# Graph attention over 16 batches: mask transfers issued from ScalarE's queue half a batch earlier, mask flags on GpSimd, one self-feature bank seeded with flags

## The chip, the cores and the metric

The kernel runs on one core of a Trainium2 chip. The metric is the device time of one execution in microseconds. Engines are named as in the profile: PE (TensorE's matmuls; PEld its weight loads), DVE (VectorE), ACT (ScalarE), POOL (GpSimd) and SP (SyncE, which here only issues transfers). A q behind an engine's name (SPq, ACTq) means its sequencer, which issues DMAs.

## The reference

Sixteen graphs of 512 nodes with 512 features. Each node attends to the first 20 nodes with 16 heads, in two directions of a labelled adjacency (11 labels):

```python
def _gat_attention(self_feat, cond_adj, label_bias, Wq, bq, Wk, bk, Wout, bout):
    kv = self_feat[:, :ng]                                  # ng = 20 of 512 nodes
    qh = (self_feat @ Wq.T + bq).reshape(B, N, H, dh)       # H = 16, dh = 32
    kh = (kv @ Wk.T + bk).reshape(B, ng, H, dh)
    aff = jnp.einsum('bnhd,bmhd->bnhm', qh, kh) * (1.0 / np.sqrt(dh))
    aff = jnp.where(cond_adj[:, :, None, :] > 0, aff, NEG) + label_bias[:, :, None, :]
    w = jax.nn.softmax(aff, axis=-1)
    out_t = jnp.einsum('bnhm,bmf->bnhf', w, kv)
    return (jnp.einsum('bnhf,hgf->bnhg', out_t, Wout) + bout.reshape(H, F // H)).reshape(B, N, F)

row_zero = v.sum(-1) == 0                                   # v: 16 x 512 x 512, q: 16 x 512
vcq = jnp.concatenate([v, jnp.where(row_zero[..., None], 0.0, q[:, None, :])], axis=-1)
self_feat = vcq @ W_self.T + b_self
output = self_feat
for d in range(2):
    A = (adj_f if d == 0 else jnp.swapaxes(adj_f, 1, 2))[:, :, :20, :]
    output = output + _gat_attention(self_feat, A.sum(-1), A @ w_bias + b_bias, ...)
return v + relu(output)
```

## The kernel before, in words

**Setup** (the first 105 us or so). The weights come in; the key rows of all batches are computed and multiplied with Wq in bursts numbered n = 0 to 21 (function `keys`), whose results (`st`, copied from PSUM by ACT and DVE) go to `g_d` in DRAM, from where each batch loads its key tensor `g`. Between the bursts stand the other setup jobs, by a table `plan` of letters, one word for a burst, and by a few lines `if n == ...`: the biases, the row sums of Wq times the bias (`bias_terms`, L671, on DVE, of the first four bursts), the value rows, self_feat of batch 0 (letter s), and the masks of batch 0 (first multiplies, count, flags, sum, spread).

**The loop.** One table `ORDER` lists the steps of a turn, each with a batch offset: `S7+0` is step S7 of this turn's batch, `F1+1` step F1 of the next one, `O-1` the last step of the batch before. The loop over turns issues the steps in that order; each engine executes its own instructions in the order in which they were issued, and semaphores are set where data passes between engines. So a step that waits holds back all that stands behind it on its engine. DMAs are issued by an engine's instruction stream too, before the change nearly all by SP; the transfers share eight completion counters in turn, and one whose counter is still in use waits for the earlier one.

**What a turn does.**
- Scores: seven half-size products S1 to S7 (`scores`, L412, 64 matmuls each) of the node features (blocks `sf`, sums `z` made by POOL in steps Z) with the keys (blocks of `g`, differences `y` made by POOL in steps Y). They are accumulated in two PSUM pairs, `pair_a` (S1, S4, S6, S7) and `pair_d` (S2, S3, S5). Before a use, a pair is seeded by ACT: `sa` (L432) and `sc` (L438) copy the bias scores `cq`, **`sd` (L436) copies the mask `both` into `pair_d`**.
- Taking the results: `t11`, `t22` (L443, ACT copies out of `pair_a`), `m22` (L452, POOL adds the mask `both`), `f11`, `f22` (L456, DVE adds `pair_d`), `t12`, `f21` (L448).
- Softmax of the four tiles 11, 12, 21, 22: maximum `mx` (L463, DVE), subtraction `sub` (L467, POOL), `exp` (L471, ACT), `sum` (L475, DVE), `rec` (L478, DVE), `nor` (L482, POOL), `turn` (L489, DVE).
- Attention: `O` (L507, PE) on banks into which ACT has copied self_feat (`so`, L493); `oe` (L518, DVE, then a DMA) adds the input and stores.
- The next batch's self_feat: seven products F1 to F7 (`product`, L279; sums `t` of the input by POOL, steps X) into PSUM `banks`: F1, F4, F6 and F7 accumulate in bank 0, F2 in bank 1, F3 and F5 in bank 2. The partial sums `p1` to `p4` (`partial`, L311, DVE) read bank 0 after F1, F6, F7 and F4, and add `nq`, which is the flag of non-zero rows times the q part (steps `nq`, L301, four ACT operations of 128x512); `j1` to `j3` (`joined`, L317, DVE) add the other banks. As bank 0 goes on being accumulated, **F6 waits for `p1`**.
- The next batch's mask: `mul0` to `mul10` (L339, ACT) multiply the eleven labels with their biases into `prod`, `cnt` (L344, DVE) counts the labels, `flg` (L347, DVE) turns the count into 0 or -9e15 in a twelfth column of `prod`, `msum` (L351, DVE) sums over the twelve, and `spr` (`mask_spread`, L362) has eight DMAs on SP that spread the sum `add` over the partitions of `both`, as the PSUM layout needs it:

```python
for pg in range(2):
    for hp in range(2):
        for t in range(2):
            nc.sync.dma_start(adds[b][bass.ts(2 * pg + hp, R), :, 2 * t : 2 * t + 2], add[bass.ts(2 * pg + t, R)])
```

In the order of the turn, S7, F1, S4, F6, F5, F7, S3, F2, F3, F4, S1, S2, S6, S5, O is PE's work from S7 on.

Of the kernel before, what the change touches and what calls it, by code (L numbers as in the profile page):

```python
# [31 lines left out]
def gat_kernel(  # L32
# [223 lines left out]
    def product(b, n):  # L256
# [12 lines left out]
        for i in range(2):  # L269
            for k in range(2):  # L270
                wide = k == 0 and n in (1, 2, 3)
                mov = x_half(b, {1: 0, 2: 1, 3: 1}[n], int(n == 3))[:, 0] if wide else x[:, k]
                for a in range(HL):
                    at = i * P + a * R
                    if isinstance(w, tuple):
                        lhs = ws_v[:, 2 * w[1] + k, bass.ds(w[0] * F // 2 + at, R)]
                    else:
                        lhs = ws_s[:, w, k, bass.ds(at, R)]
                    nc.tensor.matmul(  # L279
                        to[bass.ts(a, R), i] if wide else to[bass.ts(a, R), i, :, HK:], lhs, mov,  # L280
                        start=n in (1, 2, 5) and (i, k) == (0, 0), stop=k == 1, skip_group_check=True,
                    )
# [17 lines left out]
    def flag_row(to, b, c):  # L300
        ran(nc.scalar.activation(to, nzs[b], AF.Identity, bias=bo[:, c : c + 1], scale=qw[:, c, b : b + 1]))  # L301
# [5 lines left out]
    def partial(b, n):  # L307

        new_self(b)
        f, l = {1: (0, 0), 2: (0, 1), 3: (1, 1), 4: (1, 0)}[n]  # L310
        ran(nc.vector.tensor_add(block(b, f, l), of_bank(0), by_half(nqs[b, f])[:, :, :, l, HK:]))  # L311
# [14 lines left out]
    def first_masks():  # L326
        a = adjs[0].rearrange("p t (m l) -> p (t m) l", l=L)
        p = new_prod(0)
        nc.scalar.copy(p[:, :, :L], a)
        nc.gpsimd.tensor_mul(p[:, :, :L], p[:, :, :L], wb_sb.unsqueeze(1).to_broadcast([P, 4 * S, L]))  # L330
# [15 lines left out]
    def mask_flag(b):  # L346
        ran(nc.vector.tensor_scalar(new_prod(b)[:, :, L], conds.pop(b), 0.0, NEG, ALU.is_le, ALU.mult))  # L347
# [7 lines left out]
    def mask_spread(b):  # L355
# [3 lines left out]
        for pg in range(2):  # L359
            for hp in range(2):  # L360
                for t in range(2):
                    nc.sync.dma_start(  # L362
# [159 lines left out]
    with tc.tile_pool(name="setup", bufs=1) as sp, tc.tile_pool(name="ps_acc", bufs=4, space=PSUM) as acc["pool"]:  # L522
# [19 lines left out]
        with tc.tile_pool(name="setup_k", bufs=1) as sk:  # L542
# [132 lines left out]
            def biases():  # L675

                nc.vector.tensor_add(bqw, bqw, bq_sb)
                for hl in range(HL):
                    nc.vector.tensor_copy(bqbd[bass.ts(hl, DH), :, :, hl], bqw[bass.ts(hl, DH)])
                nc.vector.tensor_add(bo, bo_sb[:, 0], bo_sb[:, 1])  # L680
                nc.vector.tensor_add(bo, bo, bs_sb)
                nc.vector.tensor_scalar(bqn, bqbd[:, :, :2], -1.0, None, ALU.mult)
# [3 lines left out]
        with tc.tile_pool(name="setup_g", bufs=4) as sg:  # L686
# [96 lines left out]
            def self_step(b, f, h, i, k):  # L783
# [9 lines left out]
                "b": [(biases, ())],  # L793
# [9 lines left out]
            plan = "bvv vv vv ccw vv ns ssss sssw vv vv ssss ssss vv vv nww ssss ssss".split()  # L803
# [13 lines left out]
            for n, runs in enumerate(bursts):  # L817
# [12 lines left out]
                if n == 7:  # L830
                    first_masks()
                if n == 9:
                    mask_count(0)
                if n == 10:
                    load_cq(0)
                    mask_flag(0)
                if n == 11:
                    row_sums(1)
                if n == 13:
# [16 lines left out]
    with tc.manual_schedule():  # L856
# [3 lines left out]
        for t in (pair_a[:, 0], pair_a[:, 1], pair_d[:, 0], pair_d[:, 1], banks[3]):  # L860
# [4 lines left out]
            "kv": kv_copy, "cnt": mask_count, "flg": mask_flag, "msum": mask_sum, "spr": mask_spread,  # L865
            "rm": row_mask, "O": attend,
        }
        for c in range(C):
# [4 lines left out]
            steps[f"nq{c}"] = lambda b, c=c: flag_rows(b, c)  # L873
            steps[f"rs{c}"] = lambda b, c=c: row_sum(b, c)
# [19 lines left out]
        for ij in (11, 12, 21, 22):  # L894
            lower_on = nc.vector if ij in LOWER_V else nc.gpsimd
            steps[f"t{ij}"] = lambda b, ij=ij: (take_masked if ij == 12 else take)(b, ij)
# [10 lines left out]
        def first(name):  # L907
# [5 lines left out]
            if name[0] in "FXpj" or name[:2] in ("nq", "La", "LG", "Lc", "mu") or name in (  # L913
                "cnt", "flg", "msum", "spr", "kv"
# [63 lines left out]
```

## Time and profile before

| what | value |
|---|---|
| time, median of 2 runs | 643.05 us (641.56 to 644.55) |
| the profiled execution | 644.64 us, span 642.9 us |
| granted TensorE clock, mean | 0.962 |
| busy: PE, PEld, DVE, ACT, POOL | 571.8, 437.1, 453.3, 323.4, 446.6 us |
| instructions: PE, DVE, ACT, POOL | 13784, 660, 618, 380 |
| mean DMA rate | 203 GB/s |

The span is the time between the first and the last instruction that the profiler shows. Busy times of different engines overlap. In a row of the profile, "L311 DVE TENSOR_TENSOR sf<-ps_o,nq 128x492" is line, engine, operation, what is written and read, and the shape; "[1.48 <-PE ps_o L279]" is how long the engine stood idle before the instruction and what ended that; "x8" counts instructions. Batch 0 is computed in the setup, turn 0 begins at about 105 us, and the stretches of the prediction run from the end of one `O` to the end of the next, the first at 168.3 us.

### The profile page before, as it was taken

The numbers are of one execution on the slowest core, as the hardware profiler recorded it, in microseconds if no ns is written. First come the engines' busy times: TensorE is split into PE (matmuls) and PEld (weight loads), VectorE is DVE, ScalarE is ACT, GpSimd is POOL, SyncE is SP. The second block draws the span as 40 slices with busy tenths as digits, with TensorE's granted clock in tenths as the row PEclk, the third lists the DMA queues.
The fourth block names the chain that finished last, engine by engine and source line by source line (L and its number), as shares of the span: only waits on it lengthen the run. The fifth ranks groups of instructions, "written<-read, shape, count | busy, mean of one in ns | idle before, by whom it ended". The sixth has DMA issues, their size and how long they took to land.

```text
span 642.9 us, 30976 instructions
## 1 busy us (share of the span) xinstructions
PE 571.8 (89%) x13784; PEld 437.1 (68%) x13785; DVE 453.3 (71%) x660; ACT 323.4 (50%) x618; POOL 446.6 (69%) x380
## 2 busy tenths in 40 slices
PE   9979997739999899999898899999999898999952
PEld 5434444626887688777676677679877876898941
DVE  1385762417878678878785888777888787788763
ACT  1414332805656465656473756464756565664321
POOL 2304645527979687878796889787888786889841
PEclk9989999778999989999999999999999999999995
DMA  8978779975757585757575767576868575745022
GB/s 300 390 281 303 268 285 358 276 172 165 211 169 218 164 221 171 221 178 215 161 214 175 196 196 206 181 205 185 225 180 232 155 218 167 215 124 157 9 84 67
DMA packets 121031, 130.49 MB, mean 203 GB/s; under 512 B 31585, under 2 KB 93057, under 8 KB 118849
## 3 DMA queue, kind: packets, MB, share of 16 engines
q1 hardware_dynamic: 119648, 126.62, 64.5%
q8 instruction: 108, 1.77, 1.2%
q0 software_dynamic: 672, 1.36, 1.0%
q10 hardware_dynamic: 576, 0.53, 0.2%
q14 instruction: 27, 0.21, 0.1%
HBM read 85.97 MB, written 40.24 MB: 196 GB/s over the span
## 4 chain that ended last, share of the span: by engine, by line
PE 42%; DMA 16%; ACT 14%; SPq 11%; DVE 8%; issue 3%; POOL 3%; POOLq 0%; DVEq 0%; ACTq 0%
PE ps_o L279 11%; PE ps_a L412 11%; PE ps_d L412 8%; PE ps_o L507 6%; DMA xn<-in_xn 5%; SPq L362 5%; ACT prod L339 5%; DMA both<-add 3%; ACT ps_o L493 3%; DMA x<-in_xT 2%; PE ps_v L725 2%; SPq L174 2%; DMA adj<-in_adj 1%; PE ps_sf L217 1%; ACT s L471 1%
## 5 line engine op out<-in xcount | busy, mean ns | idle before, releaser
L482 POOL TENSOR_TENSOR s<-s,sum 128x640 f32<-128x640 f32 x64 | 80.9, 1274 | 55.9 <-DVE sum L478 55.8
L412 PE MATMUL ps_a<-y,z 128*32 128x152 f32 x2048 | 77.6, 302 | 19.7 <-ACT s L443 18.1
L339 ACT ACTIVATE prod<-adj,wb_sb 128x160 f32<-128x160 int32 x165 | 90.7, 589 | 7.6 <-DMA adj<-in_adj 7.6
L467 POOL TENSOR_TENSOR s<-s,top 128x640 f32<-128x640 f32 x64 | 81.5, 1275 | 16.1 <-DVE top L463 14.7
L279 PE MATMUL ps_o<-t,ws_s 128*32 128x246 f32 x1440 | 80.7, 376 | 11.7 <-DVE sf L311 11.7
L412 PEld LDWEIGHTS ps_a<-y,z 128*32 128x32 f32 x2048 | 66.9, 113 | 30.7 <-issue 28.7
L471 ACT ACTIVATE s<-s 128x640 f32<-128x640 f32 x64 | 47.0, 734 | 66.1 <-POOL s L467 66.0
L412 PE MATMUL ps_d<-g,z 128*32 128x152 f32 x2048 | 73.8, 295 | 5.0 <-ACT ps_d L438 3.3
L475 DVE TENSOR_REDUCE sum<-s 128x32 f32<-128x640 f32 x64 | 51.9, 812 | 36.1 <-ACT s L471 36.1
L279 PEld LDWEIGHTS ps_o<-t,ws_s 128*32 128x32 f32 x1440 | 54.6, 111 | 32.3 <-DVE sf L311 14.7
L412 PEld LDWEIGHTS ps_d<-g,z 128*32 128x32 f32 x2048 | 66.3, 111 | 10.9 <-ACT ps_d L438 6.3
L311 DVE TENSOR_TENSOR sf<-ps_o,nq 128x492 f32<-128x492 f32 x60 | 40.1, 668 | 36.7 <-PE ps_o L279 36.7
L507 PE MATMUL ps_o<-wt,vd 32*32 32x256 f32 x2048 | 48.0, 400 | 11.6 <-ACT ps_o L493 6.8
L279 PE MATMUL ps_o<-x,ws_v 128*32 128x256 f32 (+1 forms) x960 | 58.3, 375 | 0.0
L301 ACT ACTIVATE nq<-nz,bo,qw 128x512 f32<-128x512 f32 x64 | 51.8, 812 | 6.0 <-DVE nz L207 6.0
L489 DVE STREAM_TRANSPOSE wt<-s 128x640 f32<-128x640 f32 x64 | 53.4, 834 | 1.7 <-POOL s L482 1.6
L456 DVE TENSOR_TENSOR s<-ps_d,s 128x640 f32<-128x640 f32 x48 | 39.2, 817 | 20.3 <-POOL s L452 11.9
L436 ACT COPY ps_d<-both 128x640 f32<-128x640 f32 x16 | 11.1, 697 | 80.1 <-DMA both<-add 40.3
L463 DVE TENSOR_REDUCE top<-s 128x32 f32<-128x640 f32 x64 | 50.4, 790 | 0.0
L518 DVE SCALAR_TENSOR_TENSOR o<-ps_o,x 128x512 f32<-128x512 f32 x64 | 40.1, 670 | 11.5 <-PE ps_o L507 11.4
L493 ACT COPY ps_o<-sf 128x512 f32<-128x512 f32 x64 | 36.4, 583 | 21.7 <-DVE o L518 20.2
L507 PEld LDWEIGHTS ps_o<-wt,vd 32*32 32x32 f32 x2048 | 29.5, 105 | 25.9 <-issue 7.7
(246 smaller groups left out, 1156.6 us busy)
## 6 DMA issues: line engine op xcount, KB each, us to landing
g<-g_d SPq DMA_DIRECT2D x60, 304.0 KB, 3.3
g_d<-st SPq DMA_DIRECT2D x16, 1064.0 KB, 5.8
out_T<-o SPq DMA_DIRECT2D x64, 256.0 KB, 4.6
xn<-in_xn SPq DMA_DIRECT2D x56, 256.0 KB, 5.3
x<-in_xT SPq DMA_DIRECT2D x56, 256.0 KB, 4.2
adj<-in_adj SPq DMA_DIRECT2D x32, 440.0 KB, 4.5
vd<-bd_d SPq DMA_DIRECT2D x64, 64.0 KB, 3.3
nz<-nz_d SPq DMA_DIRECT2D x14, 256.0 KB, 4.1
```

The source lines that it names most:

```text
L279: nc.tensor.matmul(to[bass.ts(a, R), i] if wide else to[bass.ts(a, R), i, :, HK:], lhs, mov, start=n in (1, 2, 5) and (i, k) == (0, 0), st ...
L301: ran(nc.scalar.activation(to, nzs[b], AF.Identity, bias=bo[:, c : c + 1], scale=qw[:, c, b : b + 1]))
L339: ran(nc.scalar.activation(new_prod(b)[:, :, l], a[:, :, l], AF.Identity, scale=wb_sb[:, l : l + 1]))
L412: nc.tensor.matmul(to[bass.ts(q, R)], rows[:, k, q // 2, bass.ds((2 * t + u) * R, R)], keys[:, k, q % 2], start=False, stop=k == 1, skip_g ...
L463: ran(nc.vector.tensor_reduce(tops[b, ij], flat(soft_tile(b, ij)), AX.X, ALU.max))
L467: ran(engine.tensor_sub(s, s, tops.pop((b, ij)).unsqueeze(2).to_broadcast([P, 4 * 2 * HL, NG])))
L471: ran(nc.scalar.activation(s, s, AF.Exp))
L475: ran(nc.vector.tensor_reduce(tops[b, ij], flat(soft_tile(b, ij)), AX.X, ALU.add))
L482: ran(engine.tensor_mul(s, s, tops.pop((b, ij)).unsqueeze(2).to_broadcast([P, 4 * 2 * HL, NG])))
L489: ran(nc.vector.transpose(wts[b][:, j, i], soft_t.pop((b, ij)).rearrange("p v h m -> p (v h m)")))
L493: ran(nc.scalar.copy(banks[q].rearrange("p (j n) -> p j n", j=2), of_out(sfs[b], hp, pg)))
L507: nc.tensor.matmul(banks[q][bass.ts(e, DH), bass.ts(j, NH)].rearrange("p (v r) -> p v r", r=R), vds[b][r, j, e, i], w[:, :, bass.ts(block, ...
```

## The change: what moves where

1. The eight DMAs of `mask_spread` are issued by ACT instead of SP, and the step `spr` stands right behind `t22` and `Lxn0`, before `sum11`, where it stood before between `sa` and `mx21`, after F6.
2. `prod` has eleven columns instead of twelve. The flags are made in place on the count by POOL (`flg`), and a new step `madd` on POOL adds them to the sum of `msum`.
3. With `P1_A`, bank 1 is treated like the pairs (one more marking matmul ahead of the loop): ACT writes flags times q for half of the nodes into it (`nd0`, `nd1`, 128x256 each), F2 accumulates onto that, and `nq0`, `nq1` write the other half only (128x2x128). `p1` is two ACT copies (128x2x123 each) of bank 0, in place of the DVE addition.
4. In the setup `bias_terms` leaves the first four bursts for later ones (letter t), the output bias is a job of its own (letter o), biases, bias scores, masks, `row_sums(1)` and `weight_sums` move to later bursts, and the spread of batch 0 is issued by ACT at n = 18 instead of by SP at n = 15.
5. `ORDER` is written anew in many places: in turn 0 and all others `m22` stands ahead of `Y2` on POOL, and `sd` ahead of `mul0` of the next batch on ACT.

ACT around the place where the eight DMAs go, an ordinary turn, first before, then after. `s_22` is tile 22 (L443 and L460 are `t22`), `xn` the row sums, `nz` the flags, `qw` the q part, L493 and L510 are `so`, L432 and L449 `sa`.

```order
L185 ACTIVATE xn_0_2025,rs_2554<-xn_0_2025 128x512
L443 COPY s_22_2587<-ps_a 128x640 [waits DVE_49,PE_49]
L185 ACTIVATE xn_2_2069,rs_2554<-xn_2_2069 128x512 x2
L493 COPY ps_o_1174<-sf_1946 128x512 [waits DVE_49]
L432 COPY ps_a<-cq_2392 128x4x160 [waits DMAHW6_49,DMAHW5_49,DMAHW7_49,DMAHW0_49,DVE_49]
L471 ACTIVATE s_21_2639<-s_21_2639 128x640 [waits Pool_49]
L471 ACTIVATE s_22_2587<-s_22_2587 128x640 [waits Pool_49]
L339 ACTIVATE prod_2782<-adj_2517,wb_sb 128x160 [waits DMAHW6_49,DMAHW2_49]
L436 COPY ps_d<-both_2667 128x4x160 [waits DMAHW4_49,DMAHW3_49,DMAHW5_49,DMAHW2_49,DMAHW6_49,DMAHW1_49,DMAHW7_49,DMAHW0_49,DVE_49]
```

```order
L460 COPY s_22_2030<-ps_a 128x640 [waits DVE_49,PE_49]
L379 DMA both_2034<-add_1954 32x2x80 [waits DMAHW3_49,Pool_49]
L379 DMA both_2034<-add_1954 32x2x80 [waits DMAHW4_49]
L379 DMA both_2034<-add_1954 32x2x80 [waits DMAHW6_49]
L379 DMA both_2034<-add_1954 32x2x80 [waits DMAHW0_49]
L379 DMA both_2034<-add_1954 32x2x80 [waits DMAHW1_49]
L379 DMA both_2034<-add_1954 32x2x80 [waits DMAHW3_49]
L379 DMA both_2034<-add_1954 32x2x80 [waits DMAHW5_49]
L379 DMA both_2034<-add_1954 32x2x80 [waits DMAHW6_49]
L310 ACTIVATE ps_o_1173<-nz_1638,bo,qw 128x256 [waits DVE_49]
L322 COPY sf_1990<-ps_o_1172 128x2x123 [waits PE_49]
L322 COPY sf_1990<-ps_o_1172 128x2x123
```

The eight DMAs, each with a wait for its completion counter (DMAHW), now stand between `t22` and the three instructions of `nd0` and `p1`; before, ACT went on to `so` and `sa` after `t22` and two row sums, and the seed waited for all eight counters.

PE behind S4 (L412 and L429, the rows with `y_4`), first before, then after; `ps_o_1171` and `ps_o_1172` are bank 0, `ps_o_1173` and `ps_o_1174` bank 2, `t_2` marks F6, `t_1` F5, `t_3` F7:

```order
L279 MATMUL ps_o_1171<-x_2663,ws_v 32x2x123 x4
L412 MATMUL ps_a<-y_4_2760,sf_2512 32x8x19 [waits Activation_49]
L412 MATMUL ps_a<-y_4_2760,sf_2512 32x8x19 x31
L279 MATMUL ps_o_1171<-t_2_3124,ws_s 32x2x123 [waits DVE_49,Pool_49]
L279 MATMUL ps_o_1171<-t_2_3124,ws_s 32x2x123 x15
L279 MATMUL ps_o_1173<-t_1_3075,ws_s 32x2x123 x16
L279 MATMUL ps_o_1171<-t_3_3004,ws_s 32x2x123 [waits DVE_49]
```

```order
L429 MATMUL ps_a<-y_4_3876,sf_3700 32x8x19 [waits Activation_49]
L429 MATMUL ps_a<-y_4_3876,sf_3700 32x8x19 x31
L281 MATMUL ps_o_1172<-t_2_4276,ws_s 32x2x123 [waits Activation_49,Pool_49]
L281 MATMUL ps_o_1172<-t_2_4276,ws_s 32x2x123 x15
L281 MATMUL ps_o_1174<-t_1_4228,ws_s 32x2x123 [waits DVE_49]
L281 MATMUL ps_o_1174<-t_1_4228,ws_s 32x2x123 x15
L281 MATMUL ps_o_1172<-t_3_4232,ws_s 32x2x123 [waits DVE_49]
```

PE's order is the same; F6's wait has gone from DVE to ACT.

POOL in turn 0, first before, then after: `y_2` is Y2, which needs the keys `g`, and `s_22<-s_22,both` is `m22`.

```order
L254 TENSOR_TENSOR t_2_1435<-x_174,t_1_1386 128x492
L254 TENSOR_TENSOR t_4_1441<-x_174,t_2_1435 128x492
L393 TENSOR_TENSOR y_2_1464<-g_1168 128x608
L452 TENSOR_TENSOR s_22_1459<-s_22_1459,both_941 128x640
L189 TENSOR_SCALAR nz_2_1527<-rs_1431 128x4
L482 TENSOR_TENSOR s_11_1279<-s_11_1279,sum_11_1466 128x640
```

```order
L370 TENSOR_TENSOR add_1393<-add_1393,cond_1243 128x160
L256 TENSOR_TENSOR t_4_1460<-x_174,t_2_1435 128x492
L469 TENSOR_TENSOR s_22_1462<-s_22_1462,both_1024 128x640
L410 TENSOR_TENSOR y_2_1516<-g_1169 128x608
L499 TENSOR_TENSOR s_11_1278<-s_11_1278,sum_11_1475 128x640
L484 TENSOR_TENSOR s_22_1462<-s_22_1462,top_22_1543 128x640
```

`m22` has passed Y2, and `madd` (L370) has come in three places ahead of Y2.

The diff, its core:

```diff
-                wide = k == 0 and n in (1, 2, 3)
+                wide = k == 0 and n in ((1, 3) if P1_A else (1, 2, 3))
...
-                        start=n in (1, 2, 5) and (i, k) == (0, 0), stop=k == 1, skip_group_check=True,
+                        start=n in ((1, 5) if P1_A else (1, 2, 5)) and (i, k) == (0, 0), stop=k == 1, skip_group_check=True,
...
-        flag_row(nqs[b, f][:, i], b, c)
+        if P1_A and f == 0:
+            flag_row(by_half(nqs[b, f])[:, i, :, 1], b, c, 1)
+        else:
+            flag_row(nqs[b, f][:, i], b, c)
+
+    def flag_bank(b, c):
+        flag_row(banks[1].rearrange("p (i g n) -> p i g n", i=2, g=2)[:, c], b, c, 0)
...
+        if P1_A and n == 1:
+            for i in range(2):
+                ran(nc.scalar.copy(block(b, f, l)[:, i], of_bank(0)[:, i]))
+            return
         ran(nc.vector.tensor_add(block(b, f, l), of_bank(0), by_half(nqs[b, f])[:, :, :, l, HK:]))
...
-            prods[b] = msk.tile([P, 4 * S, L + 1], F32, tag="prod", name=f"prod{b}", bufs=1)
+            prods[b] = msk.tile([P, 4 * S, L], F32, tag="prod", name=f"prod{b}", bufs=1)
...
-        ran(nc.vector.tensor_scalar(new_prod(b)[:, :, L], conds.pop(b), 0.0, NEG, ALU.is_le, ALU.mult))
+        ran(nc.gpsimd.tensor_scalar(conds[b], conds[b], 0.0, NEG, ALU.is_le, ALU.mult))
...
-    def mask_spread(b):
+    def mask_add(b):
+        t = conds[b, "sum"].rearrange("p t m -> p (t m)")
+        ran(nc.gpsimd.tensor_add(t, t, conds.pop(b)))
+
+    def mask_spread(b, queue=nc.scalar):
...
-                    nc.sync.dma_start(
+                    queue.dma_start(
...
-            plan = "bvv vv vv ccw vv ns ssss sssw vv vv ssss ssss vv vv nww ssss ssss".split()
+            plan = "ovvt vvt vvt wtt vvt nst ssst ssswb vvcc vv ssss ssss vv vv nww ssss ssss".split()
...
-                    for d in range(2):
-                        bias_terms(d, n)
...
-                if n == 15:
+                if n == 17:
                     mask_sum(0)
+                if n == 18:
+                    mask_add(0)
                     mask_spread(0)
```

More of the change, by code (lines that the diff above doesn't have):

```diff
@@ L864, in gat_kernel @@
             "clr": lambda b: clear_blocks(zero), "blk": lambda b: blocks(),
[L865 removed]
+            "kv": kv_copy, "cnt": mask_count, "flg": mask_flag, "msum": mask_sum, "madd": mask_add, "spr": mask_spread,
             "rm": row_mask, "O": attend,
@@ L895, in gat_kernel @@
             lower_on = nc.vector if ij in LOWER_V else nc.gpsimd
-            steps[f"t{ij}"] = lambda b, ij=ij: (take_masked if ij == 12 else take)(b, ij)
+            steps[f"t{ij}"] = lambda b, ij=ij: (take_masked if ij == 12 or ij == 22 and T22_V else take)(b, ij)
             steps[f"m{ij}"] = lambda b, ij=ij: mask_tile(b, ij)
@@ L912, in first @@
                 return range(2, B)
-            if name[0] in "FXpj" or name[:2] in ("nq", "La", "LG", "Lc", "mu") or name in (
-                "cnt", "flg", "msum", "spr", "kv"
+            if name[0] in "FXpj" or name[:2] in ("nq", "nd", "La", "LG", "Lc", "mu") or name in (
+                "cnt", "flg", "msum", "madd", "spr", "kv"
             ):
```

45 lines of the change are left out of this document (24 added, 21 removed).

## The prediction

> **What bounds the kernel now.** First the page's busy times and its chain of work that ended last.
>
> ```profile
> PE 571.8 (89%) x13784; PEld 437.1 (68%) x13785; DVE 453.3 (71%) x660; ACT 323.4 (50%) x618; POOL 446.6 (69%) x380
> PE 42%; DMA 16%; ACT 14%; SPq 11%; DVE 8%; issue 3%; POOL 3%; POOLq 0%; DVEq 0%; ACTq 0%
> L436 ACT COPY ps_d<-both 128x640 f32<-128x640 f32 x16 | 11.1, 697 | 80.1 <-DMA both<-add 40.3
> ```
>
> TensorE (PE) is busy 89% of the span, yet the chain stands on it for only 42%: it also passes through transfers (16%), ScalarE (ACT) and SyncE's issuing (SPq, 11%). The group says where: the seed copy L436 (step `sd`), which puts the mask `both` into PSUM, waits on the mask transfers. Next, the stretches from one end of `O` to the next, a turn each.
>
> ```profile
> 363.00:393.00 30.00, 29.32 (x799) 23.35 (x790) 25.38 (x36) 19.07 (x38) 25.45 (x22) 1.00 0.72 208
> 425.50:458.00 32.50, 30.87 (x848) 27.43 (x848) 25.48 (x36) 19.15 (x39) 26.14 (x22) 1.00 0.67 189
> 554.60:584.10 29.50, 29.50 (x804) 25.83 (x808) 25.29 (x35) 17.89 (x33) 24.44 (x21) 1.00 0.61 171
> 584.10:613.20 29.10, 29.10 (x804) 25.65 (x808) 20.86 (x34) 8.63 (x13) 22.48 (x18) 1.00 0.18 55
> sum 444.90, PE 418.59 PEld 349.44 DVE 349.73 ACT 254.67 POOL 359.11; mean PE 29.90 PEld 24.96 DVE 24.98 ACT 18.19 POOL 25.65
> ```
>
> Columns: length, then busy time of PE, its loads, DVE, ACT and POOL. The 14 turns sum to 444.90, 31.8 each. The last two have no PE idle: 29.50 with all engines loaded, 29.10 as the work runs out. So a turn without stalls costs 29.5, and 14 of them 12 x 29.5 + 2 x 29.1 = 412.2: **32.7 us of the loop are stalls**. No other engine has more than 26 us of work in a turn, so they come from order. One ordinary turn, from the timeline:
>
> ```profile
> 427.75 1.35 PE L412 MATMUL ps_a<-y,z 128*32 128x152 f32 x36
> 428.91 2.02 PE L279 MATMUL ps_o<-x,ws_v 128*32 128x256 f32 x32
> 429.16 0.69 ACT L443 COPY s<-ps_a 128x640 f32<-128x640 f32 x1 [2.83 <-PE ps_a L412]
> 429.95 1.50 SPq L521 DMA_DIRECT2D out_T<-o  x3
> 430.61 2.26 PE L412 MATMUL ps_a<-y,sf 128*32 128x152 f32 x62
> 430.98 0.67 DVE L311 TENSOR_TENSOR sf<-ps_o,nq 128x492 f32<-128x492 f32 x1 [1.48 <-PE ps_o L279]
> 431.54 2.53 SPq L128 DMA_DIRECT2D xn<-in_xn  x3
> 432.82 5.16 PE L279 MATMUL ps_o<-t,ws_s 128*32 128x246 f32 x94
> 436.50 6.91 SPq L362 DMA_DIRECT2D both<-add  x8
> 444.87 0.70 ACT L436 COPY ps_d<-both 128x640 f32<-128x640 f32 x1 [5.48 <-DMA both<-add]
> ```
>
> S7 ends at 429.1 (427.75 + 1.35), ACT takes its result (`t22`, 429.16); PE does F1 and S4; F6 follows at 432.8 at once, since DVE cleared bank 0 (`p1`, 430.98) meanwhile. SP issues the eight mask transfers at 436.5 to 443.4, the seed waits 5.48 us for them, and what stands behind the seed on ACT is late: the PE stalls of this turn come after it.
>
> **The change, step by step.** *The wait it removes.* With the transfers issued at 429.2 instead of 436.5, `both` has landed long before 444. At most all 32.7 us of stalls go, at least those behind the seed; I take all but what is added below, since the turns of 29.5 show that nothing else is late.
>
> *What the eight issues cost on ACT.* Their rows on SP, and the only DMAs that ACT issues before, in setup:
>
> ```profile
> L362 SPq DMA_DIRECT2D both<-add x128: 585/596/1942, 88.0 to 595.4; - x128
> DMA to landing us min/median/max: 1.8/3.3/5.9
> L564 ACTq DMA_DIRECT2D ws_v<-in_wsT x2: 408/435/462, 0.7 to 1.2; - x2
> L564 SPq DMA_DIRECT2D xkv<-in_xkvT x4: 335/407/709, 0.7 to 5.2; - x4
> ```
>
> ACT executes in order: behind `t22` now stand eight issues, then `nd0`, then `p1` (two copies), and F6 waits for `p1` on ACT instead of DVE. Do the issues wait for `t22`'s own wait? This pair answers:
>
> ```profile
> 438.15 0.74 ACT L471 ACTIVATE s<-s 128x640 f32<-128x640 f32 x1 [0.64 <-POOL s L467]
> L339 ACTq EVENT_SEMAPHORE  x1: 17/17/17, 438.2 to 438.2; - x1
> ```
>
> The sequencer's event belonging to the next instruction is retired just after the waiting one starts, not before. So the issues start when `t22` does, 0.06 after S7's end. Eight of 0.596 with 0.04 between them take 5.1 us; the groups on SP took longer (6.91 above), since one of eight is often slow (maximum 1.942), and in the new order two of the eight wait for the completion counter of an issue five places earlier in their own group (3.2 us, against a landing of 3.3). I take 5.6, bounds 3.8 (0.435 each, the ACT row) and 7.4 (5.1 and 2.3 for SP issues in the way, below).
>
> [...]
>
> *`nd0` and `p1` on ACT.* Nearest rows:
>
> ```profile
> L301 ACT ACTIVATE nq<-nz,bo,qw 128x512 f32<-128x512 f32 x64 | 51.8, 812 | 6.0 <-DVE nz L207 6.0
> L321 ACT COPY sf<-kvn 128x80 f32<-128x80 f32 x16 | 4.3, 267 | 0.0
> L705 ACT COPY c<-ps_c 128x304 f32<-128x304 f32 x2 | 0.8, 412 | 0.8 <-PE ps_c L697 0.8
> ```
>
> A copy of 128x246 lies between 0.27 and 0.41 (0.37), `nd0` with 128x256 between 0.27 and 0.81 (0.46); less overlaps of some 0.09 between neighbours, 1.1 us for the three. Then `p1` ends 0.06 + 5.6 + 1.1 = 6.75 after S7's end. PE has F1 (1.70) and S4 (2.07) for 3.8 of it. **New stall in front of F6: s = 2.95 us a turn**, bounds 1.1 and 4.7. Nothing covers it, PE's next step is F6.
>
> *The other parts.*
>
> ```profile
> L347 DVE TENSOR_SCALAR prod<-cond 128x160 f32<-128x160 f32 x16 | 14.9, 933 | 0.0
> L189 POOL TENSOR_SCALAR nz<-rs 128x4 f32<-128x4 f32 x14 | 3.3, 232 | 0.0
> ```
>
> DVE loses the flags (0.93) and `p1` (0.67) of its 25 us. POOL gains the flags and `madd`, 128x160 each, between 0.23 (128x4, above) and 1.53 (128x640, `m22`, L452 below), about 0.56: 26.8 us in a turn of 32. On ACT `nq` is halved and `nd` takes the other half; with 5 to 7 us of issues and 0.8 of `p1` its turn holds 25 of 32. The marking matmul is one instruction in the whole program. All cost nothing while PE is the longest at 29.5; if PE ran without stalls, POOL would have 2.7 us of room left.
>
> *Startup.* Four places:
>
> ```profile
> 30.48 2.36 PE L654 MATMUL ps_k<-kvT,wk 128*32 128x320 f32 x32
> 33.19 0.69 DVE L671 SCALAR_TENSOR_TENSOR bqt<-wq_sb,br_sb 128x512 f32<-128x512 f32 x1 [4.65 <-POOL br_sb L666]
> 36.12 0.53 PE L750 MATMUL ps_g(0, 1, 1, 0, 2)1_449<-khD,wq_sb 32*128 32x304 f32 x2 [2.58 <-DVE st L770]
> 37.09 4.05 PE L654 MATMUL ps_k<-kvT,wk 128*32 128x320 f32 x32
> 114.45 0.58 ACT L339 ACTIVATE prod<-adj,wb_sb 128x160 f32<-128x160 int32 x1 [7.60 <-DMA adj<-in_adj]
> 114.94 0.69 ACT L436 COPY ps_d<-both 128x640 f32<-128x640 f32 x1
> 115.67 2.76 PE L412 MATMUL ps_d<-g,sf 128*32 128x152 f32 x40 [6.50 <-ACT ps_d L436]
> 140.44 1.46 POOL L393 TENSOR_TENSOR y<-g 128x608 f32<-128x608 f32 x1 [15.17 <-DMA g<-g_d]
> 141.86 1.53 POOL L452 TENSOR_TENSOR s<-s,both 128x640 f32<-128x640 f32 x1
> 145.60 1.87 PE L279 MATMUL ps_o<-t,ws_s 128*32 128x246 f32 x16 [11.71 <-DVE sf L311]
> ```
>
> DVE waits 4.65 for the row sums of the bias terms (L671), which holds PE 2.58, and the key rows behind it take 4.05 instead of 2.36: with L671 moved to later bursts up to 2.58 + 1.7 = 4.3 go; I take −3.5, as DVE has the same work later. The first mask spread moves from SP into ACT's stream between the copies of n = 18 and 19: 0 to +5.1, I take +2, as PE runs on until its buffers are full. The first seed `sd` stands ahead of the multiply that waited 7.60 for `adj`: 0 to −6.5, I take −1.5, because POOL prepares `z` until 115.7 in either case. In turn 0, POOL's `m22` (L452) stands behind `Y2`, which waited 15.17 for `g`, and DVE, `p1` and F6 stand behind that (PE idle 11.71); now `m22` goes first and F6, F5, F7 (5.2 us) run in the gap, less the new 2.95: 0 to −11, I take −3. Together **−6**; since the last two gaps both end at what `g` (140.4) and POOL allow, I don't add their ends and take −11 and +2 as bounds.
>
> *Sum.* Loop: 412.2 + 14 x 2.95 = 453.5, which is +8.6 on 444.9. With −6: +2.6. The profiled execution took 644.64, so 647.2; it lies 1.6 above the median of the runs, 643.05, on which the sum is 645.6. **Forecast 646.**
>
> **Rivals.** *The issues are cheap* (faster): eight at 0.435, the setup row, take 3.8 with gaps, s = 1.1, and the loop 427.6: −17.3 − 6, so 620 on the median. For it: the only ACT issues seen. Against it: the 0.585 to 0.596 of L362 hold for this very transfer shape. A second road to it is that the issues go ahead while `t22` still waits: ACT stood idle 2.83 us before `t22`, s would fall by as much to 0.1, the loop to 413.6 and the time to 606; the event at 438.2 speaks against it, and it has 0.03 of this rival's chance. [...]
>
> *The issues collide with SP's* (slower): SP issues six in the same window (429.95 and 431.54, 4.0 us), and its own group of eight took up to 6.91. If ACT's eight take 6.9, s = 4.2, the loop 471.0, the time 663; with 7.4 it is 670. It decides from s = 3.57, eight issues in 6.25 us: the 2% bound. For it: the long one in SP's groups. Against: the setup rows.
>
> *The change doesn't do what it says*: `madd` comes late on POOL, ACT stands at the first transfer with `p1` behind it, and the wait has only moved: s over 5, 675. `msum` is half a turn ahead of it, so little speaks for it.
>
> **Chances.** Forecast with s between 1.8 and 3.57: 0.55, times of 630 to 656. Cheap issues: 0.17. Collision: 0.25. Late `madd`: 0.03. Range 624 to 665: it leaves out the lower part of the first rival (0.12) and the upper of the others (0.08). Two per cent, about what a measurement of this kernel can tell, are 630.2 and 655.9: faster 0.20 (with a startup gain of −11 beside a small s), same 0.52, slower 0.28.
>
> **What would show it.** Right: `ps_d<-both` no longer waits for a transfer; PE is idle 2 to 3.5 us in front of F6 each turn, released by ACT's copy into `sf`; eight ACT issues in 5 to 6 us from the start of `t22`; turns of 32 to 33 us; the loop's first `O` some 6 us earlier. Wrong: F6 without a wait, or issues on ACT longer than 0.8 us each. What would upset all is a turn that isn't 29.5 without the seed's wait, because a further chain (the reciprocals and POOL's products ahead of `O`) is late as well.

## The result, and the profile after

The changed kernel takes 703.66 us (702.03 to 705.29) against 643.05 (641.56 to 644.55): a ratio of 1.094, 95% interval 1.079 to 1.110. It is slower by 9%; the forecast was 646 with a range up to 665. The profiled execution took 702.03. Ratios here and below leave out executions more than 1.5% above a kernel's fastest, so they can differ a little from the quotient of two medians.

The page after: busy times, the tenths of PE and its clock, the chain, and the group of F5 to F7 (L281 was L279).

```profile
PE 592.9 (85%) x13785; PEld 438.1 (63%) x13786; DVE 433.6 (62%) x629; ACT 341.6 (49%) x678; POOL 466.3 (67%) x412
PE   8999958749898979797979797979797979798972
PEclk9999989979999989899989998989998998999996
PE 63%; DMA 12%; POOL 6%; ACT 5%; ACTq 4%; DVE 4%; issue 3%; SPq 2%; POOLq 0%; DVEq 0%
L281 PE MATMUL ps_o<-t,ws_s 128*32 128x246 f32 x1440 | 105.3, 463 | 63.7 <-ACT sf L322 63.7
```

In the chain SPq has fallen from 11% to 2% and PE risen from 42% to 63%, but PE itself has got slower: the same 1440 matmuls of F5 to F7 need 105.3 us. The same group of before:

```profile
L279 PE MATMUL ps_o<-t,ws_s 128*32 128x246 f32 x1440 | 80.7, 376 | 11.7 <-DVE sf L311 11.7
```

So two things have come: 63.7 us of idle time in front of F6, which ACT's copy into `sf` ends (`p1`), and 24.6 us more for the matmuls behind it. The stretches from `O` to `O` (length, busy PE, PEld, DVE, ACT, POOL, then the granted clock), one turn and the 14 turns as one row, after; and the row of 14 turns before:

```profile
456.06:492.75 36.69, 32.20 (x804) 25.02 (x808) 23.98 (x35) 20.26 (x43) 27.18 (x24) 0.91 0.63 177
167.55:671.47 503.92, 441.33 (x11204) 349.71 (x11208) 332.35 (x461) 272.66 (x548) 375.44 (x318) 0.93 0.58 163
168.29:613.16 444.87, 418.56 (x11205) 349.40 (x11208) 349.70 (x489) 254.68 (x492) 359.12 (x290) 0.99 0.64 184
```

The loss is in the loop: 503.9 against 444.9, 4.2 us a turn, at a granted clock of 0.93 instead of 0.99. The first `O` ends at 167.55 instead of 168.29, so the startup gained 0.7 us. A clock of 0.95 or 0.91, as the single turns have it (seven turns each), is one or two stretches of 3.41 us at half speed in a turn: in the turn shown the granted clock is 0.50 from 465.57 to 472.38 us. One turn, at the place of the prediction, from the timeline after, and below it the shortest, median and longest of the matmuls F5 to F7 in ns:

```profile
458.08 2.12 PE L281 MATMUL ps_o<-x,ws_v 128*32 128x256 f32 x32
458.33 0.69 ACT L460 COPY s<-ps_a 128x640 f32<-128x640 f32 x1 [1.50 <-PE ps_a L429]
458.39 7.05 ACTq L379 DMA_DIRECT2D both<-add  x8
459.87 2.41 PE L429 MATMUL ps_a<-y,sf 128*32 128x152 f32 x64
465.50 0.57 ACT L310 ACTIVATE ps_o<-nz,bo,qw 128x256 f32<-128x256 f32 x1 [6.47 <-POOL s L484]
466.00 0.61 ACT L322 COPY sf<-ps_o 128x246 f32<-128x246 f32 x2
466.76 7.95 PE L281 MATMUL ps_o<-t,ws_s 128*32 128x246 f32 x96 [4.49 <-ACT sf L322]
L281 PE MATMUL ps_o<-t,ws_s x1440: 367/373/622, 132.8 to 652.8; 128*32 128x246 f32 x180
```

The issues begin 0.06 us after `t22`, `p1` follows them, and PE waits 4.49 us for it: the mechanism is the one forecast. New is the length of F6, F5 and F7: 7.95 us for 96 matmuls, which took 5.16 (x94) in the turn shown of before. The matmuls come in two speeds, a median of 373 ns and up to 622.

The wait that the change was to remove, and the issues on ACT's queue: shortest, median and longest in ns of all 128, and of the eight of the turn above alone.

```profile
ACT ps_d L453 <- DVE s L473: 39.8, 13, 3.8
L379 ACTq DMA_DIRECT2D both<-add x128: 592/608/1694, 93.8 to 644.3; - x128
L379 ACTq DMA_DIRECT2D both<-add x8: 592/601/609, 458.4 to 464.8; - x8
```

The seed (L453, in us, times, longest us) now waits mostly for DVE, and in no turn for a mask transfer, as forecast. Eight issues of 0.60 are 4.8 us, yet the group took 7.05: 2.2 us stand between the issues.

### The profile page after: what moved, and what is told of

Read it like the earlier page. It is cut to its first block, busy times and chain, and to the rows that moved or that the text cites. A ratio compares the mean times of both kernels' runs of the same rounds, so it can differ in the third digit from the quotient of the medians.

```text
span 700.3 us, 31021 instructions
## 1 busy us (share of the span) xinstructions
PE 592.9 (85%) x13785; PEld 438.1 (63%) x13786; DVE 433.6 (62%) x629; ACT 341.6 (49%) x678; POOL 466.3 (67%) x412
## 4 chain that ended last, share of the span: by engine, by line
PE 63%; DMA 12%; POOL 6%; ACT 5%; ACTq 4%; DVE 4%; issue 3%; SPq 2%; POOLq 0%; DVEq 0%
PE ps_o L281 25%; PE ps_a L429 13%; PE ps_d L429 12%; DMA both<-add 5%; PE ps_o L524 5%; ACTq L379 4%; PE ps_k L671 3%; DMA adj<-in_adj 2%; DMA vd<-bd_d 2%; DMA ws_q<-in_wsT 1%; ACT ps_o L310 1%; ACT nq L310 1%; PE ps_v L745 1%; ACT sf L322 1%; SPq L176 1%
## 5 line engine op out<-in xcount | busy, mean ns | idle before, releaser
L281 PE MATMUL ps_o<-t,ws_s 128*32 128x246 f32 x1440 | 105.3, 463 | 63.7 <-ACT sf L322 63.7
L281 PEld LDWEIGHTS ps_o<-t,ws_s 128*32 128x32 f32 x1440 | 62.0, 136 | 104.7 <-issue 72.8
L324 DVE TENSOR_TENSOR sf<-ps_o,nq 128x492 f32<-128x492 f32 x45 | 30.2, 670 | 106.9 <-PE ps_o L281 101.8
L488 ACT ACTIVATE s<-s 128x640 f32<-128x640 f32 x64 | 47.1, 736 | 76.3 <-POOL s L484 76.3
L429 PE MATMUL ps_a<-y,z 128*32 128x152 f32 x2048 | 74.8, 294 | 4.9 <-issue 3.8
L429 PEld LDWEIGHTS ps_a<-y,z 128*32 128x32 f32 x2048 | 65.2, 110 | 12.8 <-issue 11.0
L429 PE MATMUL ps_d<-g,z 128*32 128x152 f32 x2048 | 72.8, 293 | 0.2 <-DVE s L473 0.2
L429 PEld LDWEIGHTS ps_d<-g,z 128*32 128x32 f32 x2048 | 66.5, 110 | 2.8 <-DVE s L473 0.5
L310 ACT ACTIVATE ps_o<-nz,bo,qw 128x256 f32<-128x256 f32 x30 | 17.2, 574 | 92.5 <-DMA both<-add 54.8
L281 PE MATMUL ps_o<-x,ws_v 128*32 128x246 f32 (+1 forms) x960 | 58.6, 373 | 0.5 <-issue 0.5
L310 ACT ACTIVATE nq<-nz,bo,qw 128x512 f32<-128x512 f32 (+1 forms) x64 | 41.9, 702 | 7.6 <-DVE nz L209 7.6
L281 PEld LDWEIGHTS ps_o<-x,ws_v 128*32 128x32 f32 x960 | 35.5, 110 | 13.0 <-issue 1.8
```

What stands on the lines that cost most here:

```text
L281: nc.tensor.matmul(to[bass.ts(a, R), i] if wide else to[bass.ts(a, R), i, :, HK:], lhs, mov, start=n in ((1, 5) if P1_A else (1, 2, 5)) an ...
L310: ran(nc.scalar.activation(to, nz, AF.Identity, bias=bo[:, c : c + 1], scale=qw[:, c, b : b + 1]))
L429: nc.tensor.matmul(to[bass.ts(q, R)], rows[:, k, q // 2, bass.ds((2 * t + u) * R, R)], keys[:, k, q % 2], start=False, stop=k == 1, skip_g ...
L488: ran(nc.scalar.activation(s, s, AF.Exp))
```

## The experiments

Times are medians; the ratio to the kernel before, measured beside it on the same chip, has its 95% interval beside it. The kernel before took 639.19 us beside the four rows under the first, 642.09 beside the next four and 647.09 beside the last three, so rows of different groups compare by their ratios. "Loop" is the 14 turns of the profiled execution, 444.9 us before and 503.9 after; "first O" is where turn 0 ends, 168.3 and 167.55.

| kernel | time us | ratio (interval) | first O | loop |
|---|---|---|---|---|
| after | 703.66 | 1.094 (1.079 to 1.110) | 167.55 | 503.9 |
| after, transfers on SP | 629.68 | 0.988 (0.978 to 0.997) | 162.05 | 435.6 |
| after, issues behind `p1` | 666.83 | 1.042 (1.035 to 1.049) | 170.52 | 467.4 |
| after, PE kept busy | 676.46 | 1.058 (1.051 to 1.064) | 167.61 | 477.5 |
| after, `p1` on DVE | 636.38 | 0.993 (0.989 to 0.997) | 167.63 | 436.9 |
| before, transfers on ACT | 668.90 | 1.042 (1.037 to 1.048) | 176.15 | 461.9 |
| after, counters free | 688.03 | 1.062 (1.054 to 1.070) | 168.10 | 479.5 |
| after, first spread on SP | 702.08 | 1.092 (1.088 to 1.096) | 164.96 | 507.3 |
| after, SP and `p1` on DVE | 631.30 | 0.983 (0.981 to 0.986) | 162.05 | 439.2 |
| before, early place | 632.95 | 0.979 (0.971 to 0.987) | 166.07 | 436.8 |
| after, four and four | 631.74 | 0.979 (0.970 to 0.987) | 163.60 | 440.5 |
| after, SP and Y2 later | 632.57 | 0.982 (0.973 to 0.991) | 162.03 | 438.3 |

### The transfers back on SP

```diff
-    def mask_spread(b, queue=nc.scalar):
+    def mask_spread(b, queue=nc.sync):
```

> The changed kernel with one word changed: the eight mask transfers of every batch go back to SP's queue, at the new place behind t22. Theory A (the loss is the eight issues on ACT with their waits for completion counters ahead of nd0 and p1, 4.3 us of PE idle in front of F6, and a TensorE clock that drops after that idle time, 1.9 us): F6 no longer waits, F6 to F7 take 5.2 us again, turns of 29.5 to 30.5 us instead of 36.0; 615 to 625 us. Theory B (the new order and the work moved to ACT and POOL make the turn longer, the issues are a minor part): turns stay above 34, 680 us or more.

629.68 us, a ratio of 0.988 instead of 1.094: some 70 us below the changed kernel (68 by the ratios, 74 by the profiled executions), by one word. The group of F5 to F7 and the loop's row in this kernel:

```profile
L281 PE MATMUL ps_o<-t,ws_s 128*32 128x246 f32 x1440 | 79.2, 370 | 0.5 <-issue 0.5
162.05:597.64 435.59, 417.10 (x11205) 348.18 (x11208) 333.24 (x461) 274.59 (x546) 374.26 (x316) 1.00 0.65 188
```

No wait in front of F6, the matmuls fast again, the clock at 1.00. Theory B falls: the new order, the flags on POOL and `p1` on ACT cost nothing that shows. The expected turns were too short, though: 435.6 / 14 is 31.1, not 29.5 to 30.5, so most of the old stalls have stayed.

### PE kept busy during the wait

```diff
+WARM = 18
...
+        def keep_busy(b):
+            for _ in range(WARM):
+                nc.tensor.matmul(banks[2], marks[:, :P], marks[:, :512], start=False, stop=True, skip_group_check=True)
...
-... so3+0 Lx0+2 rs2+2 F6+1 f21+0
+... so3+0 Lx0+2 rs2+2 wm+1 F6+1 f21+0
```

> The changed kernel with 18 matmuls of zeros (128x512, bf16, into bank 2 before F5 clears it) between S4 and F6 from turn 1 on, so that PE works on while it waits for p1. The filler takes about 3.9 us at 0.22 each. Theory A's second half (F6 is slow because the clock dropped in the idle time): F6, F5 and F7 take 5.2 us instead of 6.9 on average, granted clock back above 0.95, 14 x 1.9 = 26 us less: 675 to 682 us. Rival (the group is slow for another reason, such as the transfers that run beside it): the group stays at 6.9 us, 703 us or up to 710 with the filler's own excess.

676.46 us, a ratio of 1.058 instead of 1.094, although PE does more and F6 still waits for `p1`. Timeline of one turn, the group, and the loop's row:

```profile
412.80 4.06 PE L884 MATMUL ps_o<-zero 128*128 128x512 bf16 x17
416.95 5.20 PE L282 MATMUL ps_o<-t,ws_s 128*32 128x246 f32 x96
L282 PE MATMUL ps_o<-t,ws_s 128*32 128x246 f32 x1440 | 79.5, 376 | 11.0 <-ACT sf L323 10.7
167.61:645.11 477.50, 467.92 (x11443) 372.24 (x11460) 332.09 (x461) 272.22 (x548) 374.27 (x317) 1.00 0.62 172
```

With zeros multiplied instead of idle time, F6 to F7 take 5.20 and the granted clock is 1.00. The 26.4 us that the loop gains (503.9 to 477.5) agree with the 24.6 us that the group had grown. So the slow matmuls of the changed kernel come with the idle time in front of them; the transfers beside them were the same here (172 GB/s in the loop against 163). In the loop of the changed kernel the granted clock is 0.50 in 14 stretches, one a turn, which begin between 2.9 us before and 0.9 us after the end of the wait.

### The issues behind p1

```diff
-spr+1 sum11+0 m22+0 S4+0 nd0+1 Lxn1+3 oe3-1 p1+1 rec11+0 nd1+1 Y2+1
+sum11+0 m22+0 S4+0 nd0+1 Lxn1+3 oe3-1 p1+1 rec11+0 nd1+1 spr+1 Y2+1
```

> The changed kernel with the step spr moved behind nd1, so that ACT does nd0, p1 and nd1 first and then issues the eight transfers. Theory A: no wait in front of F6, turns of 29.5 to 31 us, 615 to 635 us; what comes late instead is so and sa on ACT by some 6 us, which PE needs only for S1 and O. Theory C (any 6 us of issues on ACT cost PE some 6 us a turn, wherever they stand, as a later step of ACT is then late): turns stay at 35 to 36, 690 to 705 us.

666.83 us, between the two theories. F6 doesn't wait any more, but F3 does. One turn of this kernel:

```profile
409.18 7.60 ACTq L379 DMA_DIRECT2D both<-add  x8
416.82 0.59 ACT L510 COPY ps_o<-sf 128x512 f32<-128x512 f32 x1 [7.56 <-DMA both<-add]
419.20 1.35 ACT L488 ACTIVATE s<-s 128x640 f32<-128x640 f32 x2
419.96 0.82 DVE L492 TENSOR_REDUCE sum<-s 128x32 f32<-128x640 f32 x1 [5.85 <-ACT s L488]
420.70 0.66 DVE L324 TENSOR_TENSOR sf<-ps_o,nq 128x492 f32<-128x492 f32 x1
421.54 0.61 DVE L330 TENSOR_TENSOR sf<-ps_o,sf 128x492 f32<-128x492 f32 x1
```

Read downwards: ACT issues for 7.6 us, so the exponential (L488) is late, so DVE stands idle for 5.85 us in front of its sum, and behind the sum in DVE's order stand `p3` (L324) and `j3` (L330), which clears the bank that F3 needs. PE waited 43.5 us there, 12.9 of them in turn 0. What I had called covered isn't: with steps in a fixed order a late exponential holds work that has nothing to do with it.

### p1 on DVE, the issues on ACT

```diff
-P1_A = True
+P1_A = False
...
-nd0+1 ... nd1+1
```

> The changed kernel with P1_A = False and without the steps nd0 and nd1: p1 is one DVE addition again, F2 starts its bank itself, nq0 and nq1 are whole rows; the issues stay on ACT behind t22. Theory A: F6 waits for DVE only, so the issues no longer stand ahead of it: turns of 29.5 to 31, 615 to 635 us. Theory C (6 us of issues on ACT cost the same wherever PE meets them): 690 us or more.

636.38 us, and F6's wait is gone, as the group of F5 to F7 shows:

```profile
L281 PE MATMUL ps_o<-t,ws_s 128*32 128x246 f32 x1440 | 79.4, 370 | 0.0
308.47 3.52 PE L281 MATMUL ps_o<-x,ws_s 128*32 128x256 f32 x32 [2.44 <-DVE sf L330]
```

The issues take as long as ever (median 0.609 us), at the same place, and the loop takes 436.9 us, as with SP's queue: eight issues on ACT are dear only with `p1` behind them on ACT. That this is 30 us below the kernel with the issues behind `p1` was not expected: here the issues begin with `t22`, some 2.7 us of other ACT work earlier, and F3's wait shrinks from 43.5 us to 19.5 us, 12.2 of them in turn 0. The second row is one of the few left: F3 after 2.44 us of idle time takes 3.52 us, where it takes 1.90 otherwise.

### The queue alone, in the kernel before

```diff
-                    nc.sync.dma_start(
+                    nc.scalar.dma_start(
```

> The kernel before with one word changed: the eight transfers on ACT's queue at their old place, between sa and the exponentials of tiles 21 and 22. Theory A as it stands after the run with spr behind nd1 (six or seven us of issues on ACT hold whatever stands behind them, here the two exponentials, then DVE's sums and what DVE does behind them): the seed finds its transfers no earlier than before, the exponentials come 5 us later, turns of 32.5 to 34.5 us instead of 31.8; 650 to 680 us. Rival (ACT has room, and taking eight issues from SP gives its loads time): 635 to 645 us.

668.90 us, as theory A had it. The waits of this kernel:

```profile
ACT s L471 <- DMA both<-add: 84.0, 12, 8.2
DVE sum L475 <- ACT s L471: 57.9, 18, 6.1
PE ps_o L279 <- DVE sf L317: 30.5, 13, 4.2
```

The same chain in the old order: the exponential behind the issues, DVE's sum, `j3`, F3. It costs 17.0 us in the loop, and 7.9 come ahead of it.

### The completion counters left free

```diff
-... X3+1 msum+1 Ladj0+2 S7+0 kv+1 Lvd0+0 exp11+0 Lvd1+0 X2+1 Lvd2+0 rs0+2 Ladj1+2 Lvd3+0 oe0-1
+... X3+1 msum+1 S7+0 kv+1 exp11+0 X2+1 rs0+2 oe0-1
...
-... nd1+1 Y2+1
+... nd1+1 Lvd0+0 Lvd1+0 Lvd2+0 Lvd3+0 Ladj0+2 Ladj1+2 Y2+1
```

> The changed kernel with the six loads Ladj0, Ladj1 and Lvd0 to Lvd3, which SP issues in the 4 us before the mask transfers, moved behind nd1, so that no fresh transfer holds a completion counter that the eight need. Theory A (1.4 us of the 6.8 us from the first to the last of the eight issues are such waits): the eight take 5.2 to 5.5 us, idle time in front of F6 3.0 instead of 4.3, and with it part of the slow clock goes: 14 x 1.4 = 20 to 14 x 2.5 = 35 us less, 668 to 684 us. Rival (the time is the issuing itself, slowed by SP's issues): 6.5 us or more as before, 700 us.

The four executions took 678.2 to 692.7 us, at granted clocks from 0.945 down to 0.931. Their median, 688.03, is above the range expected; the fastest, which is the one profiled, is inside it, and so is the ratio (1.062 x 642.09 = 682). The loop is 24.4 us shorter than that of the changed kernel. One turn, and two others of this kernel with a wait of the same length:

```profile
511.75 5.59 ACTq L379 DMA_DIRECT2D both<-add  x8
518.66 5.20 PE L281 MATMUL ps_o<-t,ws_s 128*32 128x246 f32 x96 [3.27 <-ACT sf L322]
415.24 6.43 PE L281 MATMUL ps_o<-t,ws_s 128*32 128x246 f32 x96 [3.23 <-ACT sf L322]
278.83 8.05 PE L281 MATMUL ps_o<-t,ws_s 128*32 128x246 f32 x96 [3.22 <-ACT sf L322]
```

The eight issues take 5.59 us instead of 7.05 once no load of SP, issued just before, holds a counter. On average of the 14 turns the group takes 5.6 us instead of 6.8, and the gaps between its issues are 0.04 us each, where those of the changed kernel add up to 1.5 us. The wait in front of F6 falls from 4.3 to 3.3 us on average (49.5 us in 15 turns, 39.2 of them in the 12 that `p1` ends). And at this length the clock's answer varies: after 3.22 to 3.27 us of idle time the group takes 5.20, 6.43 or 8.05 us. The granted clock in the trace goes with it: 1.00 around 518.66, 0.50 for 3.41 us from 414.39 on, 0.50 for 6.83 us from 277.86 on. In the loops of this kernel and of the changed one all slow stretches have one of these two lengths and begin whole multiples of 3.41 us after one another, which suggests that the answer depends on where the wait falls on that grid.

### The first spread on SP

```diff
-                    mask_spread(0)
+                    mask_spread(0, nc.sync)
```

> The changed kernel with the spread of batch 0 alone, in the setup, back on SP. Theory A (this spread on ACT holds the copies of n = 19, which stands PE still for 7.8 us before the last burst): the first O ends near 162 instead of 167.6, the loop as it was: 696 to 699 us. Rival (the setup gains nothing else, because the keys g come at 143 us anyway and turn 0 waits for them): first O near 167, 702 to 704 us.

702.08 us, no measurable difference. The first `O` ends 2.6 us earlier (164.96), half of what theory A expected; the loop of this execution is 3.4 us longer. In the changed kernel's setup, the rows that this removes:

```profile
93.25 0.53 POOL L370 TENSOR_TENSOR add<-add,cond 128x160 f32<-128x160 f32 x1
93.81 5.25 ACTq L379 DMA_DIRECT2D both<-add  x8
99.11 1.00 ACT L788 COPY st<-s_g(3, 2, 0, 1, 2)0_1033 128x304 f32<-128x304 f32 x2 [12.19 <-DMA both<-add]
100.16 0.87 PE L770 MATMUL s_g(3, 3, 0, 0, 2)1_1071<-khD,wq_sb 32*128 32x304 f32 x2 [7.84 <-ACT st L788]
```

ACT stands at the first issue until `madd` (L370) ends on POOL, behind `weight_sums` and others, then issues: 12.19 us without a copy, of which PE feels 7.84. Without that wait PE stands still 9.15 us in turn 0 instead, at 113.47, so most of the 7.84 us is not won back.

### Transfers on SP and p1 on DVE

```diff
-    def mask_spread(b, queue=nc.scalar):
+    def mask_spread(b, queue=nc.sync):
...
-P1_A = True
+P1_A = False
```

> The changed kernel with the transfers on SP at the new place and p1 on DVE again (no nd0, nd1, P1_A = False). Where the flag bank and p1 on ACT bring nothing (as the prediction has it): the same as with the transfers on SP alone, 626 to 634 us. Where DVE's order is tight, because p1 stands in front of f22 and the maxima: 635 us or more.

631.30 us, ratio 0.983 (0.981 to 0.986), inside the interval of the SP kernel with `p1` on ACT: the flag bank and `p1` on ACT bring nothing measurable, as the prediction had it.

### The early place in the kernel before

```diff
-... oe1-1 Lxn0+3 rs2+2 Y2+1
+... oe1-1 Lxn0+3 spr+1 rs2+2 Y2+1
...
-sa+1 spr+1 mx21+0
+sa+1 mx21+0
```

> The kernel before with the step spr moved from behind sa to behind t22 and Lxn0, still on SP: the early place alone, without a new queue, new order, flags or flag bank. Theory A (the wait of the seed is what the early place removes; each of its own eight issues on SP is covered): turns near 31.1 as in the changed kernel with SP's queue, first O as before, 632 to 638 us. Rival (the whole gain of the changed kernel with SP's queue comes from the setup and the new order): 640 to 645 us.

632.95 us, ratio 0.979 (0.971 to 0.987). The old kernel with one step moved is as fast as any variant of the new one, within the intervals. Its loop is 436.8 us, so the early place brings 8.1 us there; the seed no longer waits for a transfer in any turn.

### Four on ACT, four on SP

```diff
-                    queue.dma_start(
+                    (queue if pg == 0 else nc.sync).dma_start(
```

> The changed kernel with the first four of the eight transfers on ACT and the last four on SP, at the new place. Theory A: four issues take 2.5 us, up to 4 with waits for counters, so p1 ends 3.7 to 5.1 us after S7 and PE, which has 3.8 us of other work, waits 0 to 1.3 us, too short for the clock to drop: turns of 30 to 32 us, 625 to 645 us. Rival (any issue ahead of p1 starts the loss, as queues hinder each other): half the loss of eight or more, 660 us or more.

631.74 us, ratio 0.979. Waits, the turn with the longest one, and the one turn of the loop in which the clock dropped:

```profile
PE ps_o L281 <- ACT sf L322: 9.9, 10, 2.6
234.64 5.29 PE L281 MATMUL ps_o<-t,ws_s 128*32 128x246 f32 x93 [2.58 <-ACT sf L322]
454.57 5.79 PE L281 MATMUL ps_o<-t,ws_s 128*32 128x246 f32 x73 [2.24 <-ACT sf L322]
```

Four issues fit nearly into the 3.8 us that PE has to do; the waits are 2.6 us or less, and the clock holds in all turns of the loop but one (group 80.6 us in all): after 2.24 us of idle time 73 matmuls took 5.79 us there, more than 93 did after 2.58. By the ratios half of the issues cost nothing that can be measured (0.979 against 0.988 with SP's queue), all eight some 70 us: the loss starts where the cover ends, and grows by the clock. The rival of this run falls.

### SP, with Y2 later

```diff
-... nd1+1 Y2+1 f22+0 ... sum22+0 Y4+1
+... nd1+1 f22+0 ... sum22+0 Y2+1 Y4+1
```

> The changed kernel with all transfers on SP at the new place and the step Y2 moved behind sum22, just ahead of Y4, so that in turn 0 POOL doesn't hold nor11 and the subtractions behind Y2's wait for the keys. Theory A (9.9 us of PE idle in turn 0 in front of F3 come from that): first O ends 3 to 8 us earlier, 155 to 159, turns as they were: 621 to 627 us. Rival (S4, S6 and S7 of turn 1 need the differences and the wait moves to them, or Y4 and Y3 are late in each turn): 628 us or more.

The ratio is 0.982 against 0.988: no gain clear of the noise. The wait in front of F3 in turn 0 fell from 9.9 to 5.4 us, yet the first `O` ends at 162.03 as before, so the wait moved on within turn 0, and the turns behind were not shorter. Why the time wasn't recovered in turn 0 was not followed further.

## Why the prediction was wrong, point by point

The prediction gave 647.2 for the profiled execution; it took 702.0. The 54.8 us between them, by the terms of the sum:

| term | forecast | measured | miss |
|---|---|---|---|
| wait in front of F6, 14 turns | 14 x 2.95 = 41.3 | 63.7 − 3.7 (turn 0) = 60.0 | +18.7 |
| F5 to F7 slower behind it | 0 | 105.3 − 80.7 = 24.6 | +24.6 |
| other stalls of the loop | 0 | 503.9 − 412.2 − 60.0 − 24.6 = 7.1 | +7.1 |
| startup | −6 | −0.7 | +5.3 |
| after the last of the 14 turns | 0 | 28.8 against 29.7 | −0.9 |

1. **The mechanism was right.** The issues wait for `t22`, as the event row had shown (they begin 0.06 us after it starts); they stand ahead of `p1`; F6 waits for ACT; each issue costs 0.60. The run with one word changed shows that the issues on ACT's queue are the whole loss, and the run with `p1` on DVE that they are so by standing ahead of `p1`.
2. **The step "What the eight issues cost on ACT" was mis-sized.** I took 5.6 us for the group; it took 6.8 on average of the 14 turns (5.2 to 7.6). The issues themselves were right (5.3 of the 6.8, and 0.3 for seven gaps of 0.04). What was too small is the wait for counters, the remaining 1.2: I looked only at counters reused within the group, and not at the six loads that SP issues just ahead, each of which holds a counter until it has landed, by the page after 3.8 and 4.7 us later:

```profile
adj<-in_adj SPq DMA_DIRECT2D x32, 440.0 KB, 4.7
vd<-bd_d SPq DMA_DIRECT2D x64, 64.0 KB, 3.8
```

   With those moved away the group took 5.6, and F6's wait fell by 1.0 us. So the new stall s was 4.3 us (60.0 / 14) instead of 2.95. `nd0` and `p1` took 1.1 (465.50 to 466.61), as estimated.
3. **A term was missing: the clock.** Behind idle time of 2.9 to 5.2 us F5 to F7 took 6.5 to 8.0 us in each of the 14 turns: 24.6 us that the sum put at nothing. I had the sign of it in the prediction's own startup rows: the key rows at 37.09 took 4.05 us instead of 2.36, behind 2.58 us of PE idle time, with the granted clock at 0.50 from 37.53 to 40.94, and I booked that as a gain of the setup without asking what the new stall would do. The loop of the kernel before has it too, in two of its turns: the 64 matmuls of S6 (2.27 us otherwise), beside a granted clock of 0.50 for 3.41 us from 225.27 and from 546.12 on:

```profile
224.79 3.88 PE L412 MATMUL ps_a<-y,z 128*32 128x152 f32 x64 [2.54 <-ACT s L443]
545.87 3.95 PE L412 MATMUL ps_a<-y,z 128*32 128x152 f32 x64 [2.38 <-ACT s L443]
```

   What decides whether a wait brings such a stretch on, and how long it lasts, no run shows; the multiples of 3.41 us in the kernel with the counters free only suggest that its place on that grid does. The shortest waits with the effect were of 2.0 us: F3 at 591.06 in the kernel with the issues behind `p1` took 3.14 us instead of 1.90. From there up to 3.7 us a wait had it or not (turn 0 of the changed kernel, 3.70 us, had none), and every wait above 3.70 us, in all 13 profiles from 100 us on, had it. With the 1.8 us a turn that it cost here (24.6 / 14), my own slower rival, s = 4.2 to 4.7, would have been some 688 to 695 us instead of 663 to 670.
4. **"All but what is added" of the 32.7 us was wrong the other way.** The early place on SP, in the old or the new kernel, recovers 8 to 9 us of them (444.9 to 436.8 and 435.6). The seed's wait was real, but most stalls of a turn are not behind it; a turn that isn't 29.5 without the seed's wait was what the prediction said would upset it. What they are stays open: in the SP kernel's profile the largest part of the loop's is 13.1 us in 13 waits of at most 2.1 us, put down to "issue" in front of `O`. In the changed kernel only 7.1 us of them are left, probably because the other engines catch up while PE waits for `p1`; no run tests that.
5. **Startup.** With SP's queue the first `O` ends 6.2 us earlier, where the sum without its +2 for ACT's first spread has 8; 2.2 of them come with the early place alone (166.07). With ACT's queue the first spread costs PE 7.84 us on the spot, as it had to wait for `madd` behind POOL's `weight_sums`, but the first `O` only 2.6 us by the run without it, so the +2 was near. The other 2.9 us (164.96 against 162.05) belong to turn 0's own eight issues, behind which F6 waits there too (3.70 us in the changed kernel). The terms −3.5, −1.5 and −3 were not tested one by one.
6. **The other rivals.** That the issues collide with SP's was priced by SP's group (6.9), and the group did take 6.8, but for another reason: ACT's issues were not longer beside SP's (0.608 median against 0.596 on SP), the waits came from the shared counters. The 2.3 us for SP issues in the way, which the bound of 7.4 held, no run shows. The 2% bound of that rival was miscounted: by the sum it is s = 3.68, and 3.57 gives 654 us. Cheap issues (0.435) did not occur. The flags, `madd` and the flag bank cost nothing, as forecast.

## What to carry to other kernels

Here a DMA issue was work of the engine that issued it: eight of 0.6 us, with waits for counters that other queues' transfers held, stood for 6.8 us in front of everything that ACT did next, and in a kernel whose steps have a fixed order a late engine delays its readers' unrelated work too (43.5 us in front of F3 with the issues behind `p1`). Issue transfers from an engine on which nothing urgent stands behind them, or in portions that fit into the cover, or move the urgent step to another engine: each of the three brought the changed kernel down to 630 to 636 us. And a wait of PE isn't worth its length alone: in this case some waits from 2.0 us on, and all above 3.7, slowed the matmuls behind them, and in the loop of the changed kernel each of 2.9 to 5.2 us went with a granted clock of 0.50 for 3.41 or 6.83 us, 1.8 us more a turn. Add that, and distrust a forecast that rests on a wait which may have it or not, as those between the two lengths here.

## What had not been expected of the hardware

The same wait of 3.2 us gave 5.20, 6.43 and 8.05 us for the same 96 matmuls in one execution. Two of 2.0 us slowed the matmuls behind them, one of 3.70 didn't. Filling the wait with multiplications of zeros made the loop 26.4 us shorter while PE did more. And eight issues split over two queues side by side cost each no more than on one (median 0.59 and 0.61 us).
